# Selective scan on one Trainium2 core: the scan's last states copied by ScalarE, and the sum over directions made by identity products

## The chip, the core and the metric

The kernel runs on one core of a Trainium2 chip. The core has five instruction queues that run beside each other and meet through semaphores: TensorE (PE in the profile; its weight loads are PEld), VectorE (DVE), ScalarE (ACT), GpSimd (POOL) and SyncE (SP), which here issues the DMA transfers. Each queue runs its instructions in the order of the program. SBUF is the large on-chip memory; PSUM is the small one that TensorE writes its products to, and VectorE and ScalarE read and write it too.

The metric is the device time of one execution in microseconds (us), the median of several runs. The profile is one further execution, recorded by the hardware.

## What is computed

The reference is a network of two layers on 8 images of 128 channels and 64 x 64 places. The change touches the first layer's mixer alone, which runs a selective scan in four directions and sums the results:

```python
xp = x_norm @ in_w.T                                   # 4096 places, 128 channels
x_tb = xp.reshape(b, h, w, D).swapaxes(1, 2).reshape(b, L, D)
U = jnp.stack([xp, jnp.flip(xp, 1), x_tb, jnp.flip(x_tb, 1)], 0)
Y = jax.vmap(_mamba)(U, ...)                           # once for each direction

# in _mamba, for each direction: xh, z, dt, Bm, Cm are made from u, and then
h = exp(dt_t[..., None] * A) * h + (dt_t * x_t)[..., None] * B_t[:, None, :]
y = einsum('bdn,bn->bd', h, C_t)                       # 16 states a channel
y = (y + xh * Dp) * silu(z)
return y @ out_w.T

y_fused = gate[0] * y_lr + gate[1] * y_rl + gate[2] * y_tb + gate[3] * y_bt
out = skip_gate * (y_fused @ out_w.T) + (1.0 - skip_gate) * skip
```

Directions 1 and 3 read the sequence backwards, directions 2 and 3 read the image column by column. Their results are turned back before they are summed. Behind this come an expert layer and a whole second layer, which stay as they are.

## The kernel before

**Tiling.** The first layer is written by `scan_blocks` (L703). It goes through 8 images, in each through 4 directions `d`, in each through 4 chunks `j` of 1024 places, and in each chunk through 16 groups of 8 channels x 16 states = 128 partitions. A group of a chunk is a slot `n`; there are 2048 slots. The text numbers slots within their chunk, 0 to 15.

**A slot.** Slot `n` works ahead for its followers. For slot n+1 TensorE spreads dt over the states: six bf16 products into `dA` (two halves of 512 places, three bf16 parts each), and ScalarE takes the exponential in place. `dA` is a PSUM tile of two banks with two buffers. For slot n+2 GpSimd multiplies `xE` by B into `bx`; for slot n+4 SyncE fetches `xE`. For slot n itself VectorE runs the scan in place in `dA` (L765), starting from the column of `last` that the previous chunk left, then multiplies by C into `hc` (L335, the helper of all tensor-by-tensor operations), then copies the last column of `dA` into `last` for the next chunk (L772, helper L347). The fourth chunk of a direction copies nothing, so there are 3 x 16 x 32 = 1536 such copies. Every fourth slot TensorE sums the states of four `hc` tiles into the y bank (`y<-hc,kt`).

**The steps of a chunk.** What a chunk needs besides is a table of steps (L587) with the slot at which each is issued, counted from the chunk's first slot. Steps of several chunks and of the next image's input (`input_steps`, L605, in 8 of the 16 chunks of an image, for all but the last image) fall into one slot. Those that matter here, by the slot within a chunk in which they fall:

- slot 0: the products of D with x into the y bank (`skip`, 16), a dt product (`dt_product`), and a table load of ScalarE
- slot 1: `gate_y` (17): VectorE multiplies the y bank (two PSUM banks, 1024 places) by `zs`, the gated z
- slot 2: `out_product` (17.5: at the head of the slot, ahead of the slot's dA products) multiplies `zs` by the output weights and overwrites the y bank; `out_add` (18) brings the two halves of the y bank into `r`, the sum over directions that stays in SBUF. ScalarE also has softplus steps of a later chunk here (`plus_one`, `relu_abs`)
- slots 3 and 4: VectorE's and ScalarE's remaining softplus steps (`lost`, `ln`, `dt`)
- slots 4 to 6: the products that spread B and C and their copies by ScalarE
- slots 7 to 14: z products, z gates, convolution products (`taps`), x gates; in slot 12 of a direction's first chunk VectorE also makes `D_diag`.

`m` is a PSUM tile of one bank with two buffers, through which all the small products go; `y` has one buffer.

**The sum over directions.** For direction 0, `out_add` copies the y bank to `r` by ScalarE (L583). For the others VectorE adds it to `r` in place (L585, again shown as L335): forwards in order, reversed for d = 1, and through a view with a step of 64 elements (256 bytes) for d = 2 and 3, reversed for d = 3. `image_steps` (L676) adds the residual to `r` by GpSimd and stores it.

**What sets the order.** The tile framework sets the semaphores from what each instruction reads and writes. Besides, `ordered` (L307) chains the instructions of each engine, so that every queue runs exactly in the order in which the slots issue them:

```python
def ordered(self, i):
    if self.order is not None:
        e = i.ins.engine
        if e in self.order:
            self.after(i, self.order[e])
        self.order[e] = i
    return i
```

Within slot n the order of issue is: the steps at its head, the dA products and the exponential of slot n+1, `bx`, the fetch of `xE`, the scan, the C product and the copy of slot n, the y products, the other steps.

Of the kernel before, what the change touches and what calls it, by code (L numbers as in the profile page):

```python
# [12 lines left out]
ALU = mybir.AluOpType  # L13
# [9 lines left out]
L = 4096  # L23
S = 512
# [5 lines left out]
CH = 1024  # L30
NCH = L // CH
# [238 lines left out]
def bc(ap, n, axis=None):  # L270

    axis = len(ap.shape) if axis is None else axis
    v = ap.unsqueeze(axis)
    shape = list(v.shape)
    shape[axis] = n
    return v.to_broadcast(shape)


class Net:
# [167 lines left out]
    def scan_steps(self, ch, xp, r, pl, ps):  # L447
# [4 lines left out]
        nc, d, j = self.nc, ch["d"], ch["j"]  # L452
        pool = nc.gpsimd
        back = d % 2 == 1
        lo = L - CH * (j + 1) if back else CH * j
        dtb, cb2 = self.w(f"dt_b{d}"), self.cb2[:, d : d + 1]
        start = [lo + (1 - q if back else q) * S for q in range(2)]
        half = [slice(q * S, (q + 1) * S) for q in range(2)]
        ID, TANH = AF.Identity, AF.Tanh
        v = {}  # L460

        def order(ap):
            return ap[:, ::-1] if back else ap
# [5 lines left out]
        def make(name, bufs, width=S):  # L469
            t = v[name] = pl.tile([C, width], F32, name=name.rstrip("01"), bufs=bufs)  # L470
            return t
# [4 lines left out]
                o = start[q] + (6 - t if back else t)  # L476
                self.mm(p, self.Wt[:, d, t, :], xp[:, o : o + S], start=t == 0, stop=t == 3)

        def gate(name, to, q, **kw):
            p = v[f"{name}{q}"]  # L480
            self.act(order(to[:, half[q]]), p, ID, scale=0.5, **kw)
            th = make(f"th{q}", 2)
            self.act(order(th), p, TANH, scale=0.5, **kw)
            self.act(th, th, ID, bias=self.k("one"))

        def gated(of, name, q):
            to = of[name][:, half[q]]
            self.tt(to, to, v[f"th{q}"], ALU.mult, pool)

        def x_gate(q):  # L490
            if q == 0:
                ch["xs"] = make("xs", 3, CH)
            gate("x", ch["xs"], q, bias=cb2)

        def z_product(q):
            self.mm(bank(f"z{q}"), self.w(f"z_w{d}"), xp[:, start[q] + PAD : start[q] + PAD + S])
# [1 line left out]
        def z_gate(q):  # L498
            if q == 0:
                make("zs", 1, CH)  # L500
            gate("z", v["zs"], q)

        def dt_product(q):
            self.mm(bank(f"d{q}"), self.Wd[:, d, :], ch["xs"][:, half[q]])
# [58 lines left out]
                self.mm(ch["y"][rows_, half[q]], self.D_diag[:, rows_], ch["xs"][:, half[q]], start=False)  # L563

        def gate_y():
            self.tt(v["zs"], ch["y"], v["zs"], ALU.mult)

        def out_product(q):
            self.mm(ch["y"][:, half[q]], self.Wo[:, d, :], v["zs"][:, half[q]])

        def out_add(q):
            p, lo = ch["y"][:, half[q]], CH * j + q * S
            lo = L - S - lo if back else lo
            if d < 2:
                to = r[:, lo : lo + S]
                to = to[:, ::-1] if back else to
            else:
                w0 = lo // 64
                to = r.rearrange("p (h w) -> p w h", w=64)[:, w0 : w0 + S // 64, :]
                to = to[:, ::-1, ::-1] if back else to  # L580
                p = p.rearrange("p (w h) -> p w h", h=64)
            if d == 0:
                self.ordered(nc.scalar.copy(to, p))  # L583
            else:
                self.tt(to, to, p, ALU.add)  # L585

        table = [  # L587
            (-23, taps, 0, (0, 1)), (-22, taps, 0, (2, 3)), (-21, taps, 1, (0,)), (-20, taps, 1, (1,)),
            (-19, taps, 1, (2, 3)), (-21, x_gate, 0), (-18, x_gate, 1), (-20, gated, ch, "xs", 0), (-17, gated, ch, "xs", 1),
            (-16, dt_product, 0), (-15, dt_product, 1), (-16, self.table, EXP_LN_SET),  # L590
            (-15, relu_abs, 0), (-15, exp, 0), (-14, plus_one, 0), (-14, relu_abs, 1), (-13, exp, 1), (-13, plus_one, 1),
# [111 lines left out]
    def scan_blocks(self, r, xp, xt, pl, ps):  # L703

        nc = self.nc
        chunks = [{"d": d, "j": j} for b in range(self.nb) for d in range(4) for j in range(NCH)]
        per = NQ * 4 * NCH  # L710
        todo, ahead = {}, {}

        def plan(at, steps):
            for rel, step, *args in steps:
                slot = int(np.ceil(at + rel))
                (todo if slot == at + rel else ahead).setdefault(slot, []).append((step, args))

        for i, s in enumerate(range(NS)):
            plan(-56 - 7 * (NS - 1 - i), self.input_steps(0, s, xp, pl, ps, {
                "px": ("xE", 4), "pxc": ("hc", 5), "psq": ("bx", 4), "var": ("xs", 3), "q": ("C16", 2)}))  # L720
        plan(-24, [(0, self.table, EXP_TANH_SET)])
        for b in range(self.nb):
            plan(per * b, self.image_steps(b, r, xp, xt, pl))
            if b + 1 < self.nb:
                for i, s in enumerate((2, 3, 4, 5, 6, 7, 0, 1)):
                    plan(per * b + NQ * (5 + i), self.input_steps(b + 1, s, xp, pl, ps))
        for i, ch in enumerate(chunks):
            plan(NQ * i, self.scan_steps(ch, xp if ch["d"] < 2 else xt, r, pl, ps))
        total = NQ * len(chunks)
        self.order = {}  # L730
        self.table(EXP_LN_SET)
        total = NQ * len(chunks)
        self.order = {}
        self.table(EXP_TANH_SET)
        xE, bx, dA, hcs = {}, {}, {}, {}
        last = None
        for n in range(min(todo), max(todo) + 1):
            for step, args in ahead.pop(n, ()):
                step(*args)
            u = n + 1  # L740
            if 0 <= u < total:

                ch, q = chunks[u // NQ], 4 * (u % 4) + u % NQ // 4
                dA[u] = ps.tile([128, CH], F32, tag="dA", bufs=2, name="dA")
                sel = self.expand[:, 8 * q : 8 * q + 8, :].rearrange("p c n -> p (c n)")
                for h in range(2):
                    sg = slice(h * S, (h + 1) * S)
                    for i in range(3):
                        self.mm(dA[u][:, sg], sel, ch["parts"][:, i, sg], start=i == 0, stop=i == 2)
                self.act(dA[u], dA[u], AF.Exp, scale=self.negA[:, ch["d"] * NQ + q : ch["d"] * NQ + q + 1])  # L750
            u = n + 2
            if 0 <= u < total:
                bx[u] = pl.tile([128, CH], F32, name="bx", bufs=4)
                self.tt(bx[u], xE.pop(u), chunks[u // NQ]["B16"], ALU.mult, nc.gpsimd)
            u = n + 4
            if 0 <= u < total:
                ch, q = chunks[u // NQ], 4 * (u % 4) + u % NQ // 4
                xE[u] = pl.tile([128, CH], F32, name="xE", bufs=4)
                nc.sync.dma_start(xE[u], bc(ch["dtx"][8 * q : 8 * q + 8, :], NST, 1))
            if 0 <= n < total:  # L760
                ch, q = chunks[n // NQ], 4 * (n % 4) + n % NQ // 4
                if n % NQ == 0 and ch["j"] == 0:
                    last = pl.tile([128, NQ], F32, name="last", bufs=2)
                t = dA.pop(n)
                self.ordered(nc.vector.tensor_tensor_scan(  # L765
                    out=t, data0=t, data1=bx.pop(n), initial=0.0 if ch["j"] == 0 else last[:, q : q + 1],
                    op0=ALU.mult, op1=ALU.add,
                ))
                hcs[n] = pl.tile([128, CH], F32, name="hc", bufs=5)
                self.tt(hcs[n], t, ch["C16"], ALU.mult)  # L770
                if ch["j"] < NCH - 1:
                    self.copy(last[:, q : q + 1], t[:, CH - 1 :], nc.vector)  # L772
            if n % 4 == 0 and 4 <= n < total + 4:
                g0 = n - 4
                ch, k = chunks[g0 // NQ], g0 % NQ // 4
                if k == 0:
                    ch["y"] = ps.tile([C, CH], F32, tag="y", bufs=1, name="y")
                for h in range(2):
                    for g in range(4):
                        self.mm(ch["y"][32 * g : 32 * g + 32, h * S : (h + 1) * S],  # L780
                                self.k("collect")[:, 32 * k : 32 * k + 32],
                                hcs[g0 + g][:, h * S : (h + 1) * S], start=k == 0, stop=False)
                for g in range(4):
                    del hcs[g0 + g]
            for step, args in todo.pop(n, ()):
                step(*args)
        self.order = None
        self.silus_done([])
# [1127 lines left out]
```

## Time and profile before

| | us |
|---|---|
| median of 3 runs (18311.58 to 18333.5) | 18323.12 |
| the profiled execution | 18312.49 |
| its span in the profile | 18310.7 |
| first slot's scan starts, last slot's scan ends | 120.7, 8513.2 |

The groups of the page and of the trace that the change touches:

| operation | engine | count | busy, us | mean of one, ns |
|---|---|---|---|---|
| scan from a last state | VectorE | 1536 | 3609.4 | 2350 |
| scan from zero | VectorE | 512 | 1172.2 | 2289 |
| C product `hc` | VectorE | 2048 | 2508.0 | 1225 |
| copy of the last state | VectorE | 1536 | 226.5 | 147 |
| `gate_y` | VectorE | 128 | 155.4 | 1214 |
| add to `r` | VectorE | 192 | 196.9 | 1070 |
| copy to `r`, direction 0 | ScalarE | 64 | 34.2 | 591 |
| exponential | ScalarE | 2048 | 2229.6 | 1089 |
| output product | TensorE | 512 | 252.3 | 615 |

A group's busy time is the time in which one of its instructions ran, and the mean is that of one instruction. Instructions overlap: one can be issued before the one ahead of it has ended, so starts show the pace and durations do not. A product of fp32 operands of 512 columns is two matmul instructions. A row of the timeline gives the start, the length, the engine, the line, the operation with what it writes and reads, and how many were merged; in brackets stand the engine's idle time before it and what ended it.

### The profile page before, as it was taken

Reading aid. Unit: us, or ns where it says so; the run is one execution under the profiler, and the core shown is the slowest. Engines: PE = TensorE matmul, PEld = TensorE weight load, DVE = VectorE, ACT = ScalarE, POOL = GpSimd, SP = SyncE. Lnnn points to the kernel's source line nnn. Section 1 sums busy time; section 2 is a strip of 40 time slices with the busy share of each in tenths; the row PEclk is TensorE's granted clock in tenths of the full one; section 3 lists DMA queues with packets and bytes.
Section 4 is the critical chain, followed back from the end, with each engine's and each line's share of the span. In section 5 each row is a group of like instructions: output and inputs, shape, how many; then the busy total and the mean of one; then the engine's idle time right before and its main releaser. Section 6 shows DMA issues by size and latency. Waiting matters only on the chain. (4 is left out here: it accounts for less than half of the span.)

```text
span 18310.7 us, 298654 instructions
## 1 busy us (share of the span) xinstructions
PE 15555.4 (85%) x113015; PEld 8270.0 (45%) x114072; DVE 15183.5 (83%) x20469; ACT 11216.3 (61%) x15914; POOL 9304.0 (51%) x6309
## 2 busy tenths in 40 slices
PE   7777777777777777776687999999999999998998
PEld 2222222222222222223344677777777777774443
DVE  7999999999999999998464777777777777777886
ACT  5656666565666656554353677677767776776553
POOL 7878788787878788774111222222222222222444
PEclk9999999999999999998797999999999999998999
DMA  4555555555555555554541111111111111111222
GB/s 131 143 143 146 146 145 141 147 144 144 145 144 145 141 148 143 145 136 118 160 147 53 30 29 31 31 31 29 31 31 30 30 31 31 29 31 41 93 95 82
DMA packets 818996, 1735.35 MB, mean 95 GB/s; under 512 B 183571, under 2 KB 383667, under 8 KB 809139
## 3 DMA queue, kind: packets, MB, share of 16 engines
q1 hardware_dynamic: 817558, 1716.18, 32.8%
q8 instruction: 902, 14.78, 0.3%
q14 instruction: 536, 4.39, 0.1%
HBM read 1474.55 MB, written 241.30 MB: 94 GB/s over the span
## 5 line engine op out<-in xcount | busy, mean ns | idle before, releaser
L335 POOL TENSOR_TENSOR bx<-xE,B 128x1024 f32<-128x1024 f32 x2048 | 4808.6, 2357 | 342.8 <-DMA xE<-dtx_d 184.6
L288 PE MATMUL dA<-parts,expand 128*128 128x512 bf16 x11777 | 3168.4, 400 | 1753.3 <-DVE last L347 1307.1
L296 ACT ACTIVATE dA<-dA,negA 128x1024 f32<-128x1024 f32 x2048 | 2229.6, 1089 | 2962.2 <-PE dA L288 2954.8
L765 DVE TENSOR_TENSOR_SCAN dA<-dA,last,bx 128x1024 f32<-128x1024 f32 x1536 | 3609.4, 2350 | 91.2 <-ACT dA L296 78.5
L288 PEld LDWEIGHTS <-expand 128*128 128x128 bf16 x12288 | 1127.3, 100 | 4149.5 <-DVE last L347 2120.1
L344 DVE SCALAR_TENSOR_TENSOR E_cm<-E_cm,gm_cm 128x1024 f32<-128x1024 f32 x2048 | 2440.5, 1227 | 280.9 <-ACT E_cm L296 268.4
L335 DVE TENSOR_TENSOR hc<-dA,C 128x1024 f32<-128x1024 f32 x2048 | 2508.0, 1225 | 107.8 <-DVE dA L765 2.3
L1292 POOL COPY Sd_cm<-S_cm 64x128 f32<-64x128 f32 x1024 | 879.2, 859 | 2625.6 <-DVE S_cm L335 2536.6
L296 ACT ACTIVATE E_cm<-ss_p 128x1024 f32<-128x1024 f32 x2048 | 1980.7, 1021 | 267.5 <-PE ss_p L288 184.6
L335 POOL TENSOR_TENSOR xD_cm<-tok_cm,D_cm 128x256 f32<-128x256 f32 x512 | 404.2, 789 | 2377.2 <-PE y_p L288 2309.0
L288 PE MATMUL y_p<-E_cm,pad_cm 128*32 128x128 f32 x32768 | 1321.2, 277 | 119.8 <-DVE E_cm L344 118.6
L765 DVE TENSOR_TENSOR_SCAN dA<-dA,bx 128x1024 f32<-128x1024 f32 x512 | 1172.2, 2289 | 49.4 <-ACT dA L296 43.2
L288 PE MATMUL ss_p<-ssB_cm,ssA_cm 128*128 128x512 bf16 x3582 | 1041.0, 383 | 114.5 <-DVE gm_cm L335 45.9
L288 PE MATMUL y<-hc,kt 128*32 128x512 f32 x8192 | 1077.8, 646 | 3.7 <-DVE hc L335 3.6
L288 PEld LDWEIGHTS y_p<-E_cm,pad_cm 128*32 128x32 f32 x32768 | 903.6, 110 | 369.2 <-DVE E_cm L344 202.8
L288 PE MATMUL bc_p<-stk_cm,W_cm 128*128 128x256 f32 x4096 | 943.7, 384 | 26.3 <-DMA stk_cm<-in_ones_dram 20.6
L1149 DVE COPY dtr_cm<-tok_p 128x16 f32<-128x16 f32 x1024 | 176.5, 172 | 867.3 <-ACT tok_cm L296 867.3
L288 PEld LDWEIGHTS bc_p<-stk_cm,W_cm 128*128 128x128 f32 x4096 | 771.2, 191 | 167.5 <-issue 28.3
L288 PE MATMUL tok_p<-W_cm,stk_cm 128*128 128x200 f32 x4096 | 749.5, 336 | 0.0
L344 DVE SCALAR_TENSOR_TENSOR dw<-h,w_second,dw 128x512 f32<-128x512 f32 x1024 | 723.0, 748 | 1.2 <-ACT h L296 0.8
L296 ACT ACTIVATE tok_cm<-tok_p 128x384 f32<-128x384 f32 x1024 | 502.2, 490 | 347.8 <-DVE dtr_cm L1149 183.9
L288 PEld LDWEIGHTS tok_p<-W_cm,stk_cm 128*128 128x128 f32 x4096 | 683.1, 190 | 52.2 <-ACT BC_cm L296 48.1
(432 smaller groups left out, 29346.0 us busy)
## 6 DMA issues: line engine op xcount, KB each, us to landing
xE<-dtx_d SPq DMA_DIRECT2D x2048, 512.0 KB
dtx_d<-dtx SPq DMA_DIRECT2D x256, 256.0 KB
x<-x SPq DMA_DIRECT2D x256, 256.0 KB
pb<-p_d SPq DMA_DIRECT2D x64, 1024.0 KB
ssA_cm<-cs_cm SPq DMA_DIRECT2D x3072, 4.0 KB
stk_cm<-xs SPq DMA_DIRECT2D x368, 128.0 KB
stk_cm<-y SPq DMA_DIRECT2D x368, 128.0 KB
w<-in_w_dram SPq DMA_DIRECT2D x32, 1024.0 KB
```

The source lines that it names most:

```text
L288: return self.ordered(self.nc.tensor.matmul(out, lhsT=lhsT, rhs=rhs, start=start, stop=stop))
L296: i = self.ordered(self.nc.scalar.activation(out, in_, func, **kw))
L335: self.ordered((eng or self.nc.vector).tensor_tensor(out, a, b, op))
L344: self.ordered(self.nc.vector.scalar_tensor_tensor(out=out, in0=a, scalar=s, in1=b, op0=op0, op1=op1))
L765: self.ordered(nc.vector.tensor_tensor_scan(out=t, data0=t, data1=bx.pop(n), initial=0.0 if ch["j"] == 0 else last[:, q : q + 1], op0=ALU. ...
L1149: nc.vector.tensor_copy(dtr[:, c, jj, :], v[:, :, cfg.wsil :])
L1292: nc.gpsimd.tensor_copy(Sd[gr, :, g * hi : (g + 1) * hi], S2[gr])
```

## The change

Two things are changed, both in the first layer.

1. The last state is copied by ScalarE (`nc.scalar.copy`), and the copy is issued between the scan and the C product instead of behind the product by VectorE.
2. The sum over directions is made in the y bank: behind each output product a second product, by the identity, adds the old values of `r` to the same bank (directions 1 to 3), and ScalarE copies the bank to `r` in all directions. `r` is read and written in its own order, so the reversal of directions 1 and 3 moves ahead: `z_gate` no longer reverses, the halves of `zs` are swapped, and `gate_y` reads the y bank reversed.

```diff
-        def gate(name, to, q, **kw):
+        def gate(name, to, q, order=order, **kw):
             p = v[f"{name}{q}"]
-            self.act(order(to[:, half[q]]), p, ID, scale=0.5, **kw)
+            self.act(order(to), p, ID, scale=0.5, **kw)
...
         def gated(of, name, q):
-            to = of[name][:, half[q]]
+            to = of[name][:, half[1 - q if back and name == "zs" else q]]
...
-            gate("z", v["zs"], q)
+            gate("z", v["zs"][:, half[1 - q if back else q]], q, lambda ap: ap)
...
         def gate_y():
-            self.tt(v["zs"], ch["y"], v["zs"], ALU.mult)
+            self.tt(v["zs"], order(ch["y"]), v["zs"], ALU.mult)
+
+        def rows_of(ap, q):
+            at = lo + q * S
+            if d < 2:
+                return ap[:, at : at + S]
+            return ap.rearrange("p (h w) -> p w h", w=64)[:, at // 64 : (at + S) // 64, :]
+
+        def out_bank(q):
+            p = ch["y"][:, half[q]]
+            return p if d < 2 else p.rearrange("p (w h) -> p w h", h=64)
 
         def out_product(q):
-            self.mm(ch["y"][:, half[q]], self.Wo[:, d, :], v["zs"][:, half[q]])
+            self.mm(ch["y"][:, half[q]], self.Wo[:, d, :], v["zs"][:, half[q]], stop=d == 0)
+            if d:
+                self.mm(out_bank(q), self.k("ident"), rows_of(r, q), start=False)
 
         def out_add(q):
...
-            if d == 0:
-                self.ordered(nc.scalar.copy(to, p))
-            else:
-                self.tt(to, to, p, ALU.add)
+            self.ordered(nc.scalar.copy(rows_of(r, q), out_bank(q)))
...
                     op0=ALU.mult, op1=ALU.add,
                 ))
+                if ch["j"] < NCH - 1:
+                    self.ordered(nc.scalar.copy(last[:, q : q + 1], t[:, CH - 1 :]))
                 hcs[n] = pl.tile([128, CH], F32, name="hc", bufs=5)
                 self.tt(hcs[n], t, ch["C16"], ALU.mult)
-                if ch["j"] < NCH - 1:
-                    self.copy(last[:, q : q + 1], t[:, CH - 1 :], nc.vector)
```

More of the change, by code (lines that the diff above doesn't have):

```diff
@@ L492, in x_gate @@
                 ch["xs"] = make("xs", 3, CH)
-            gate("x", ch["xs"], q, bias=cb2)
+            gate("x", ch["xs"][:, half[q]], q, bias=cb2)
         def z_product(q):
@@ L565, in gate_y @@
         def gate_y():
-            self.tt(v["zs"], ch["y"], v["zs"], ALU.mult)
+            self.tt(v["zs"], order(ch["y"]), v["zs"], ALU.mult)
[7 more added lines that the diff above has]
+            return p if d < 2 else p.rearrange("p (w h) -> p w h", h=64)
         def out_product(q):
-            self.mm(ch["y"][:, half[q]], self.Wo[:, d, :], v["zs"][:, half[q]])
+            self.mm(ch["y"][:, half[q]], self.Wo[:, d, :], v["zs"][:, half[q]], stop=d == 0)
+            if d:
+                self.mm(out_bank(q), self.k("ident"), rows_of(r, q), start=False)
         def out_add(q):
[L572 to L576, printed above, removed]
-            else:
[L578 to L581, printed above, removed]
-            if d == 0:
-                self.ordered(nc.scalar.copy(to, p))
-            else:
-                self.tt(to, to, p, ALU.add)
+            self.ordered(nc.scalar.copy(rows_of(r, q), out_bank(q)))
         table = [
```

## The prediction

> **What bounds the kernel now.** First the page's header and its forty slices: is one engine full, and where?
>
> ```profile
> span 18310.7 us, 298654 instructions
> PE 15555.4 (85%) x113015; PEld 8270.0 (45%) x114072; DVE 15183.5 (83%) x20469; ACT 11216.3 (61%) x15914; POOL 9304.0 (51%) x6309
> ...
> DVE  7999999999999999998464777777777777777886
> ACT  5656666565666656554353677677767776776553
> ```
>
> The first layer is slices 1 to 19. There VectorE is full and ScalarE is not; asked for 110 to 8560 us, the table of windows gives VectorE 8139.6 of 8450 us (96%), TensorE 6587.9, GpSimd 6699.1, ScalarE 5089.2. So one reads VectorE's order next. The change touches this layer alone. Its 2048 slots (8 images x 4 directions x 4 chunks x 16 groups) take 4.10 us from scan to scan, 65.6 us a chunk. A slot with nothing extra looks so in the timeline:
>
> ```profile
> 3044.12 2.29 DVE L765 TENSOR_TENSOR_SCAN dA<-dA,bx 128x1024 f32<-128x1024 f32 x1
> ...
> 3044.26 1.47 PE L288 MATMUL dA<-parts,expand 128*128 128x512 bf16 x6
> ...
> 3045.77 1.09 ACT L296 ACTIVATE dA<-dA,negA 128x1024 f32<-128x1024 f32 x1 [0.47 <-PE dA L288]
> ...
> 3046.45 1.23 DVE L335 TENSOR_TENSOR hc<-dA,C 128x1024 f32<-128x1024 f32 x1
> ...
> 3047.59 0.15 DVE L347 COPY last<-dA 128x1 f32<-128x1 f32 x1
> 3047.65 2.29 DVE L765 TENSOR_TENSOR_SCAN dA<-dA,bx 128x1024 f32<-128x1024 f32 x1
> ```
>
> Scan and C product stand back to back; the copy of the last state lasts 0.15 us, but the scan after it starts 0.06 us behind it. The next slot's chain (matmuls, exponential) starts when the product frees a dA buffer and ends at 3046.86, **0.41 us after** this slot's product began. Nobody minds, as VectorE does not need it before 3047.65: two dA buffers hide that chain. Hold on to that 0.41.
>
> **Part 1: the copies of the last state.** 1536 leave VectorE. Their price there is not 226 us (1536 x 147 ns) but about 0.065 us each in start times (3.59 us a plain slot in chunks 1 and 2 against 3.52 in chunk 3, which copies nothing): 100 us gained at most.
>
> What is added is a reader of dA on another engine, between the scan and the product. Does the product then wait for it? Neither writes what the other reads. The second layer has just such a pair: ScalarE and VectorE read different columns of tok_p, a PSUM tile.
>
> ```profile
> 12007.98 0.49 ACT L296 ACTIVATE tok_cm<-tok_p 128x384 f32<-128x384 f32 x1 [0.54 <-PE tok_p L288]
> 12008.50 0.18 DVE L1149 COPY dtr_cm<-tok_p 128x16 f32<-128x16 f32 x1 [2.06 <-ACT tok_cm L296]
> 12008.71 1.05 ACT L296 ACTIVATE tok_cm<-tok_p 128x384 f32<-128x384 f32 x2 [0.24 <-DVE dtr_cm L1149]
> 12009.24 0.17 DVE L1149 COPY dtr_cm<-tok_p 128x16 f32<-128x16 f32 x1 [0.56 <-ACT tok_cm L296]
> ```
>
> The reads alternate strictly, in the order of the program, 0.03 us apart; ScalarE's second read waits for VectorE's first although it takes the other half of the tile (512 such waits in the tile's view, one for each second read). [...] So the product waits for ScalarE's copy.
>
> And that copy is queued **behind the exponential of the next slot**. Behind it stand the slot's own ScalarE steps and the exponential after that; behind the waiting product, VectorE's steps and the next scan. In the slot above, without the VectorE copy the matmuls start 0.06 earlier, the exponential ends at 3046.80. The copy's own time is not in the trace: 0.15 us as on VectorE, 0.205 as ScalarE's 128x4 row; I take 0.2, less the 0.07 by which ScalarE's instructions overlap (3042.45 + 1.09 against the next start at 3043.47). Then 0.03 to VectorE: product at 3046.96 instead of 3046.45. Less the copy's 0.06 the plain slot goes from 3.59 to about **4.03** (0.05 + 1.51 + 1.09 + 0.13 + 0.03 + 1.22): a loop through three engines instead of VectorE alone.
>
> Whatever delays matmul or exponential now stalls VectorE. From one product's end to the next, in slots of a copying chunk (now: scan starts averaged over chunks 0 to 2):
>
> - slots 5, 7, 9, 10, 11, 13, 14, 15: 29.1 us together, then 8 x 4.03: **+3.2**.
> - slot 0: TensorE has y products, D products and a dt product between two dA groups (3000.33 to 3006.26). 3.6, then 5.9: **+2.3**.
> - slot 1: gate_y 1.2, then both output products 1.8 ahead of the matmuls 1.5, exponential 1.1, copy, product. 5.45, then 7.0: **+1.5**.
> - slot 2: ScalarE must do the copy-out and three softplus steps (3.0 us; in 7 of 16 chunks also two powers, 1.2) before the exponential. Average 5.2, then 5.6: **+0.4**.
> - slot 3: VectorE's own softplus steps (2.7) cover the chain: **0**.
> - slot 4: the logarithm waits for the scan through the copy ahead of it, with two input steps in front in 7 of 16 chunks: **+0.5**.
> - slot 6: the second C spread product waits for a bank that ScalarE empties after its copy; with input steps 1.1 more: **+1.2**.
> - slots 8 and 12: y products and another product, 2.7 to 2.9 us against 2.5 of free TensorE: **+0.8** and **+0.5** (D_diag included).
>
> Sum 10.4 us a chunk.
>
> **Part 2: the sum over directions.** 192 adds leave VectorE: 0.64 us each in direction 1, 1.23 in directions 2 and 3.
>
> ```profile
> 3007.69 1.22 DVE L335 TENSOR_TENSOR zs<-y,zs 128x1024 f32<-128x1024 f32 x1
> ...
> 3008.96 1.98 PE L288 MATMUL y<-zs,W_out 128*128 128x512 f32 x4 [0.38 <-DVE zs L335]
> ...
> 3010.78 1.46 PE L288 MATMUL dA<-parts,expand 128*128 128x512 bf16 x6
> ...
> 3012.28 1.09 ACT L296 ACTIVATE dA<-dA,negA 128x1024 f32<-128x1024 f32 x1 [1.05 <-PE dA L288]
> ...
> 3012.49 2.45 DVE L335 TENSOR_TENSOR r<-r,y 128x512 f32<-128x512 f32 x2
> ...
> 3014.85 2.29 DVE L765 TENSOR_TENSOR_SCAN dA<-dA,bx 128x1024 f32<-128x1024 f32 x1
> ```
>
> The adds run beside a chain that ends at 3013.37, so without them the scan gains 1.5 us here, not 2.4. Direction 0, which adds nothing, shows what remains: slots 1 to 4 take 21.1 us (chunk 2), direction 1 21.5, directions 2 and 3 22.5; part is given back in slot 3, where ScalarE is late. The two identity products stand ahead of those matmuls: 4 instructions, 1.8 us at the price of the output products. In a chunk without copies of states that takes the gain back: about +1.0 in direction 1, 0 in 2 and 3. In a copying chunk they stand inside the loop: +1.8 in slot 1 in three of four directions, **+1.4** on average. What lay behind the adds is in slot 2's 5.2 already.
>
> [...] In directions 2 and 3 the identity product reads r every 256 bytes. The nearest row is the add with that stride: 1.23 for 0.64, two strided streams at 2.4 ns an element. TensorE takes 1.8 ns an element even contiguous (0.91 us for 512). [...] I take 0 for TensorE and keep 116 for the range. For ScalarE's strided write I take half a microsecond a copy over direction 0's 0.59, between 0 and 0.6; it is in slot 2.
>
> The reversal moved to gate_y, and the swapped halves of zs, cost nothing: the reversed adds of direction 1 took 0.64, no more than a forward 128x512 product (0.69); above, a doubling would be 64 x 1.2 = 77 us. No DMA moves. GpSimd adds the residual to r and SP stores r as before; GpSimd has a fifth of the layer free, more in longer slots.
>
> **Sum.** 10.4 + 1.4 = 11.8 us x 96 copying chunks = 1133; the other 24 chunks with an add: 8 x 1.0 = 8. The profiled execution took 18,312.5 us (span 18,310.7): 19,454. The median is 18,323, 11 more; I say **19,460 us**.
>
> **Rivals.**
> - *The readers are not ordered* (8%). Then VectorE gains 100 us, part 2 costs 1.0 x 32 = 32: 18,245, faster. It decides once the product starts at the scan's end. Against it: 512 waits at tok_p.
> - *The copy finds ScalarE free* (8%): only 0.03 + 0.2 + 0.03 - 0.06 a slot, 1536 x 0.2 = 307, plus 32: 18,650. Against it: the 0.41 above.
> - *TensorE cools* (7%). After 4.9 us of waiting six dA matmuls took 2.74 us (3018.51), not 1.47. [...] But groups of slots 0 and 1 average 1.8 now, after pauses of 2 us. If the 8 plain slots pay 1.27 each: 975 more, 20,430.
>
> **Chances.** The forecast keeps 77%, by itself 19,050 to 19,900 (116 for the stride, cold groups in three slots, some 370; less if copy and hand-offs are shorter). The range 18,900 to 19,950 reaches towards its neighbours. A measurement can tell about 0.2%, 37 us. The first rival is split between faster (7%) and the same (2%); all else is slower, 91%.
>
> **What would show it.** In the profile after: C products with idle time ended by ScalarE's copy, plain slots near 4.0 us, exponential, copy and product in a row, VectorE's busy share of the layer near 80%, output-product slots the longest. Products still at the scan's end would prove part 1 wrong; a group of four identity matmuls over 1.8 us, the stride.

## The result, and the profile after

| | before, us | after, us |
|---|---|---|
| median of 4 runs each | 18327.81 | 19574.38 |
| the profiled execution's span | 18310.7 | 19572.4 |
| first slot's scan to last slot's scan | 8390.2 | 9667.5 |
| a chunk whose slots copy states (mean of chunks 0 to 2) | 65.9 | 78.2 |
| a chunk whose slots copy none (chunk 3) | 64.7 | 67.5 |

The changed kernel is slower by 6.8%: ratio 1.0683, 95% interval 1.067 to 1.0697. The first layer grew by 1277 us and the whole span by 1262, so all of it is there. The last two rows are means of the scan starts in the traces.

The same parts of the page as before, its header and the forty slices (first layer: slices 1 to 20):

```profile
span 19572.4 us, 300377 instructions
PE 16127.2 (82%) x114456; PEld 8417.4 (43%) x114456; DVE 14852.7 (76%) x18741; ACT 11492.9 (59%) x17642; POOL 9307.0 (48%) x6309
...
DVE  6788788787887878788846567777777777776886
ACT  5555555555555555555426466777677677776553
PEclk8999999999998999999979799999999999999999
```

VectorE has lost the nines that marked it as the bound, and no other row has gained them: the layer is bound by no engine now, but by waiting between engines. VectorE is busy for 80% of it (6775.7 of 8450 us), the share that the prediction named. VectorE's work shrank by 331 us (15183.5 to 14852.7) and the kernel grew by 1262. What it waits for stands in the costliest groups of the page, first before, then after. The last columns are busy time, mean length in ns, and the engine's idle time ahead of the group with what ended it:

```profile
L335 DVE TENSOR_TENSOR hc<-dA,C 128x1024 f32<-128x1024 f32 x2048 | 2508.0, 1225 | 107.8 <-DVE dA L765 2.3
```

```profile
L335 DVE TENSOR_TENSOR hc<-dA,C 128x1024 f32<-128x1024 f32 x2048 | 2508.5, 1225 | 1673.8 <-ACT last L769 1646.9
```

The C product is no shorter or longer than before (1225 ns), but VectorE stood idle ahead of it for 1674 us, where before that was 108 us. The waits view counts 1536 such waits: one for each copied state. A plain slot in the timeline of the kernel after:

```profile
3349.91 2.35 DVE L764 TENSOR_TENSOR_SCAN dA<-dA,last,bx 128x1024 f32<-128x1024 f32 x1
3350.05 1.45 PE L288 MATMUL dA<-parts,expand 128*128 128x512 bf16 x6 [0.81 <-DVE hc L335]
...
3351.54 1.09 ACT L296 ACTIVATE dA<-dA,negA 128x1024 f32<-128x1024 f32 x1 [1.07 <-PE dA L288]
3352.56 0.16 ACT L769 COPY last<-dA 128x1 f32<-128x1 f32 x1
3352.75 1.23 DVE L335 TENSOR_TENSOR hc<-dA,C 128x1024 f32<-128x1024 f32 x1 [0.49 <-ACT last L769]
3353.89 2.35 DVE L764 TENSOR_TENSOR_SCAN dA<-dA,last,bx 128x1024 f32<-128x1024 f32 x1
```

Read it as a staircase: the previous product ends just before 3350, the matmuls start, then the exponential, then the copy, then the product. The scan ended at 3352.26, but the product began at 3352.75, behind a copy that stands in ScalarE's queue behind the exponential (and starts 0.07 us before that one's end). Scan to scan is 3.98 us, against 3.59 in the plain slots of chunks 1 and 2 before (3.53 in the slot shown of before, which is one of a first chunk).

And the output products of a chunk of direction 2 or 3, with old values of `r` added by TensorE:

```profile
3386.84 1.04 PE L288 MATMUL y<-zs,W_out 128*128 128x512 f32 x2
...
3387.71 1.87 PE L288 MATMUL y<-r,kt 128*128 128x512 f32 x2
...
3390.92 1.09 ACT L296 ACTIVATE dA<-dA,negA 128x1024 f32<-128x1024 f32 x1 [3.83 <-PE dA L288]
...
3392.11 2.36 DVE L764 TENSOR_TENSOR_SCAN dA<-dA,last,bx 128x1024 f32<-128x1024 f32 x1 [3.68 <-ACT dA L296]
...
3393.12 1.90 ACT L584 COPY r<-y 128x512 f32<-128x512 f32 x2
```

The identity product, two instructions like the output product, takes 1.87 us where that takes 1.04. The scan waited 3.68 us for an exponential that stands behind two output products and two identity products. (This output step falls into a chunk that copies no states, so the waiter is the scan and not the C product.)

### The profile page after: what moved, and what is told of

It reads as the page before. It is cut to its first block, busy times and chain, and to the rows that moved or that the text cites. A ratio compares the mean times of both kernels' runs of the same rounds, so it can differ in the third digit from the quotient of the medians.

```text
span 19572.4 us, 300377 instructions
## 1 busy us (share of the span) xinstructions
PE 16127.2 (82%) x114456; PEld 8417.4 (43%) x114456; DVE 14852.7 (76%) x18741; ACT 11492.9 (59%) x17642; POOL 9307.0 (48%) x6309
## 5 line engine op out<-in xcount | busy, mean ns | idle before, releaser
L288 PE MATMUL dA<-parts,expand 128*128 128x512 bf16 x12288 | 3279.4, 407 | 2230.8 <-DVE hc L335 2226.8
L335 DVE TENSOR_TENSOR hc<-dA,C 128x1024 f32<-128x1024 f32 x2048 | 2508.5, 1225 | 1673.8 <-ACT last L769 1646.9
L288 PE MATMUL ss_p<-ssB_cm,ssA_cm 128*128 128x512 bf16 x4096 | 1088.5, 383 | 70.6 <-DVE gm_cm L335 44.5
L288 PE MATMUL y<-hc,kt 128*32 128x512 f32 x8192 | 1131.9, 675 | 2.1 <-DVE hc L335 2.1
L335 POOL TENSOR_TENSOR dtx<-sp_r,xs 128x512 f32<-128x512 f32 x256 | 324.4, 1267 | 1071.8 <-DVE sp_r L335 1071.1
```

The source lines that it names most:

```text
L288: return self.ordered(self.nc.tensor.matmul(out, lhsT=lhsT, rhs=rhs, start=start, stop=stop))
L335: self.ordered((eng or self.nc.vector).tensor_tensor(out, a, b, op))
```

## The experiments

The prediction named two parts. The theory: the loss is the C product's wait for a copy that is queued behind the next exponential; the sum over directions costs little beside it. The rivals: the read order itself costs, or the second part costs as much. The first four runs share their runs of the kernel before (median 18319.4); the next four share theirs (18309.14); the last has 18322.24.

| run | us | ratio to before, 95% interval |
|---|---|---|
| part 1 alone | 19383.4 | 1.0578 (1.056 to 1.0595) |
| part 2 alone | 18623.4 | 1.0163 (1.0146 to 1.018) |
| part 1, exponential behind the copy | 18637.4 | 1.0173 (1.0156 to 1.019) |
| part 1, copy behind the product | 18517.8 | 1.0106 (1.009 to 1.0123) |
| part 1, copy untied | 18327.2 | 1.0011 (1.0002 to 1.0021) |
| part 2, no identity products | 18326.4 | 1.0009 (1.0 to 1.0019) |
| part 2, identity products contiguous | 18506.3 | 1.0108 (1.0093 to 1.0124) |
| before, copy by ScalarE in light slots | 18249.2 | 0.9971 (0.9959 to 0.9982) |
| part 2, no identity products, r contiguous | 18292.6 | 0.9988 (0.9977 to 0.9998) |

**Part 1 alone.** Against the kernel before:

```diff
+                if ch["j"] < NCH - 1:
+                    self.ordered(nc.scalar.copy(last[:, q : q + 1], t[:, CH - 1 :]))
                 hcs[n] = pl.tile([128, CH], F32, name="hc", bufs=5)
                 self.tt(hcs[n], t, ch["C16"], ALU.mult)
-                if ch["j"] < NCH - 1:
-                    self.copy(last[:, q : q + 1], t[:, CH - 1 :], nc.vector)
```

> Part 1 alone: the last states copied by ScalarE between scan and product, the sum over directions as before. Theory (the product waits for a copy that stands behind the next exponential): plain slots at 4.0 us as in the changed kernel, 11.1 us more in a copying chunk as its chunks of direction 0 show, 96 x 11.1 = 1070 us: about 19,400. Rival (the loss comes as much from the identity products inside the loop): well under 19,000.

1064 us more than before, as the theory had it. The second part adds only 191 us to this (19574.4 less 19383.4).

The longest step of a copying chunk is the one that holds the output products: from the end of product 1 to the end of product 2 it takes 8.2 us, against 5.4 before. The product's wait makes `gate_y` late, so TensorE waits too, and then runs slower:

```profile
2862.08 3.15 PE L288 MATMUL y<-zs,W_out 128*128 128x512 f32 x4 [2.80 <-DVE zs L335]
...
2865.02 2.04 PE L288 MATMUL dA<-parts,expand 128*128 128x512 bf16 x6
```

The same four output products took 1.98 us before, after a wait of 0.38 (3008.96). The table of windows gives the granted clock as the third number from the end, here for the output products before and in this run:

```profile
3008.96:3010.94 1.98, 1.98 (x5) 0.87 (x6) 1.98 (x1) 1.95 (x4) 0.15 (x1) 1.00 0.52 190
```

```profile
2862.08:2865.00 2.92, 2.92 (x4) 0.98 (x5) 2.21 (x1) 0.00 (x0) 0.63 (x1) 0.62 0.53 148
```

Over all copying chunks the output products take 2.70 us for 1.96 and the matmuls behind them 2.06 for 1.50 up to the exponential, at a mean granted clock of 0.75 and 0.76, where both had 1.00 before. That is 1.3 us a copying chunk, some 125 of the 1064 us. In the plain slots the clock stays at 1.00.

**Part 2 alone.** The changed kernel with the copies of the kernel before.

> Part 2 alone: sum by identity products, the last states copied by VectorE behind the product as before. By the prediction's sum 32 us, with the stride's doubling (identity products at 1.04 us an instruction in directions 2 and 3) some 150 us: 18,360 to 18,480. Rival (by the chunks of the changed kernel that copy nothing, which grew by 2.7 us in direction 1 and some 4 in 2 and 3): about 18,660, so more is lost at the output products than these products' own time.

304 us more: near the rival's number, not the prediction's. Where it loses, by slots (means of chunk 2): slot 2 went from 5.24 to 6.33 us, as the adds went and the identity products came, and slot 3 from 6.46 to 7.65, where the prediction had nothing for part 2. Slot 3 is also why part 2 is dearer by itself than on top of part 1 (191): in a copying chunk with part 1 it takes 6.4 us from product to product, with part 2 and without, so that its 1.2 us in 96 chunks, 116 us, are not lost there.

**Part 1, the exponential behind the copy.** In slot n, the exponential of slot n+1 is issued after the copy and not before the scan:

```diff
-                self.act(dA[u], dA[u], AF.Exp, scale=self.negA[:, ch["d"] * NQ + q : ch["d"] * NQ + q + 1])
+            exp_of = u
...
                     self.ordered(nc.scalar.copy(last[:, q : q + 1], t[:, CH - 1 :]))
+            if 0 <= exp_of < total:
+                ce, qe = chunks[exp_of // NQ], 4 * (exp_of % 4) + exp_of % NQ // 4
+                self.act(dA[exp_of], dA[exp_of], AF.Exp, scale=self.negA[:, ce["d"] * NQ + qe : ce["d"] * NQ + qe + 1])
+            if 0 <= n < total:
                 hcs[n] = pl.tile([128, CH], F32, name="hc", bufs=5)
```

> Part 1 alone, with the exponential of the next slot issued behind the copy instead of ahead of it. Theory (the price is the place behind the exponential): the product waits only for copy and hand-offs, plain slots 3.75 to 3.85 us, in sum 0.2 to 0.25 us for 1536 slots plus late ScalarE steps: 18,650 to 18,800. Rival (the order of the two reads itself costs what is lost, wherever the exponential stands): no nearer than 19,300.

Two instructions of one engine change places and 746 of the 1064 us are gone. The order of the two reads is still there, and a slot looks so:

```profile
3163.53 0.16 ACT L770 COPY last<-dA 128x1 f32<-128x1 f32 x1 [0.96 <-DVE dA L765]
3163.60 1.09 ACT L296 ACTIVATE dA<-dA,negA 128x1024 f32<-128x1024 f32 x1
3163.73 1.23 DVE L335 TENSOR_TENSOR hc<-dA,C 128x1024 f32<-128x1024 f32 x1 [0.23 <-ACT last L770]
```

Now ScalarE waits for the scan and copies at once; the product waits 0.23 us for copy and hand-offs, and the exponential runs beside it. Plain slots take 3.72 us, less than was expected. So the place in ScalarE's queue is most of the price, and the read order about 0.13 us a slot, after the 0.06 that VectorE saves. What else remains of the 318 us, over a third, lies mostly in slot 4 (5.98 for 4.92) and slot 7 (4.22 to 4.49 for 3.70), where ScalarE's steps come later than before.

**Part 1, the copy behind the product.** The kernel before, with its `self.copy(..., nc.vector)` made `self.ordered(nc.scalar.copy(...))` in its old place.

> Part 1 alone, with ScalarE's copy issued behind the C product. Theory (it is VectorE's wait that costs): VectorE waits for nobody, plain slots 3.52 us; the next matmuls in that dA buffer and ScalarE's steps wait 0.2 us longer, which two buffers hide: 18,200 to 18,400. Rival (ScalarE held up to the product's end makes exponentials late): over 18,500.

A miss for the theory as it was put: 198 us slower, the rival's side. No product waits any more and plain slots take 3.53 us, less than before, as expected. But the waits of VectorE show a new line-up:

```profile
DVE dA L765 <- ACT last L772: 214.4, 251, 3.3
DVE m L335 <- ACT sp_u L296: 123.7, 96, 2.0
DVE m L344 <- ACT sp_u L296: 85.1, 104, 0.8
```

(us in total, times, longest.) ScalarE is now held up to the end of the product, its softplus steps of slots 3 and 4 start later, and VectorE waits for those: slot 4 takes 6.2 us instead of 4.9, slot 3 7.0 instead of 6.4. Slot 7 takes 4.3 to 4.7 instead of 3.7, largely because of the first line. There the scan waits for an exponential that ScalarE reaches late; the view names the copy since that ended last (at 2642.43 in one such slot, the exponential at 2642.34, and the scan began at 2642.44). Elsewhere scans begin before the copy ahead of them, so they do not depend on it. A wait was taken from one engine and put on the other.

**Part 1, the copy untied.** Part 1 alone with `self.negA[:, q : q + 1]` copied in place of the column of `t`.

> Part 1 alone with the tie cut: ScalarE's copy stands where the change puts it, but reads a column of a constant in SBUF, so it waits for no scan and no product waits for it. The scan's state is not passed from chunk to chunk. Theory (the whole price is the product's wait): VectorE rid of 1536 copies at 0.065 us, 18,170 to 18,260. Rival (one more instruction on ScalarE makes exponentials and softplus steps late by itself): 18,320 or more.

The same 1536 instructions in the same place, and of 1064 us over the kernel before 18 are left (18327.2 less 18309.1): the tie is the loss. The gain that the theory put on top did not come, so the time is the rival's. Plain slots did go from 3.59 to 3.53 us, but slots 4 and 7 gave it back (5.23 for 4.92, 3.9 to 4.0 for 3.7), and so did slot 12 of the first chunks (5.78 for 5.16). VectorE's 100 us were worth nothing here, since one more ScalarE instruction stands ahead of steps that VectorE waits for: ahead of its scans it waited 184.6 us for ScalarE's exponential and copy (132.1 and 52.5), against 121.6 before.

**Part 2 without the identity products.**

```diff
-            self.mm(ch["y"][:, half[q]], self.Wo[:, d, :], v["zs"][:, half[q]], stop=d == 0)
-            if d:
-                self.mm(out_bank(q), self.k("ident"), rows_of(r, q), start=False)
+            self.mm(ch["y"][:, half[q]], self.Wo[:, d, :], v["zs"][:, half[q]])
```

> Part 2 alone without the identity products: directions are not summed, each overwrites r. Theory (part 2 loses by the 1.8 to 2.8 us of TensorE ahead of the next dA products): without them the adds' gain is left, 18,220 to 18,270. Rival (ScalarE's copies to r, ahead of its softplus steps, make those late and VectorE wait in slot 3): 18,350 or more.

Between the two: 17 us over the kernel before. Taking 197 us of adds off VectorE gained nothing. Slot 2 fell by 1.0 us (5.24 to 4.28 in chunk 2) and slot 3 rose by 1.2 (6.46 to 7.67). The waits of VectorE say to whom it went, first before, then in this run:

```profile
DVE m L344 <- ACT sp_u L296: 24.4, 53, 0.6
```

```profile
DVE m L344 <- ACT sp_u L296: 186.9, 126, 2.5
```

That is the softplus step waiting for ScalarE, which has the two copies to `r` ahead of its own softplus steps.

**Part 2 without identity products, `r` written without a step.** The same, with `r[:, lo + q * S : lo + q * S + S]` as the copy's target.

> Part 2 alone without the identity products, and ScalarE writing r without a step in all directions (directions are not summed, and 2 and 3 land in other places). Theory (ScalarE's strided copies at 1.09 us stand ahead of its softplus steps and make slot 3 long): 64 chunks times 2 copies times 0.5 us less than the run without identity products, about 64 us: 18,250 to 18,280. Rival (the two copies' place is enough, their length does not matter): 18,310 to 18,340.

34 us less, between theory and rival (against their own runs of before: 17 more and 30 less). Slot 3 of directions 2 and 3 fell by 0.7 us (8.54 to 7.82 in direction 2, chunk 2). Direction 1, whose copies are short in both runs, keeps its 7.82. So both count: the place of the copies (slot 3 of direction 1 took 6.44 us before), and the half microsecond by which the step lengthens each.

**Part 2, identity products contiguous.** Part 2 alone with `r[:, lo + q * S : lo + q * S + S]` as the moving operand.

> Part 2 alone, the identity products of directions 2 and 3 reading r without a step (other places are added than the reference adds); ScalarE still writes r with the step of 256 bytes. Theory (the step doubles these products and they stand in VectorE's way): 64 chunks times 1.9 us less than part 2 alone, 18,480 to 18,530. Rival (the added TensorE time of the step is hidden, ScalarE's strided writes cost the rest): 18,600.

117 us less than part 2 alone, or 107 when each is set against its own runs of the kernel before. First the instructions' lengths in the view of the tile `r`, of the changed kernel (shortest, median, longest in ns), then the same row of this run:

```profile
L288 PE MATMUL y<-r,kt x384: 592/1033/1061, 497.2 to 9803.5; 128*128 128x512 f32 x192
```

```profile
L288 PE MATMUL y<-r,kt x384: 592/592/593, 453.9 to 8715.8; 128*128 128x512 f32 x192
```

The step of 256 bytes lengthens the instruction from 592 to 1033 ns, and all of it lands on the time: 256 instructions in directions 2 and 3 times 0.44 us are 113 us. Part 2 alone is so taken apart, each run against its own runs of before: 17 us with the copies moved, 180 for the products themselves (18506.3 less 18326.4), 107 for their step, in sum 304.

**A faster version.** The kernel before with the copy by ScalarE, behind the product, where a slot has little ScalarE work that VectorE waits for:

```diff
-                    self.copy(last[:, q : q + 1], t[:, CH - 1 :], nc.vector)
+                    if n % NQ in (5, 8, 9, 10, 11, 12, 13, 14, 15):
+                        self.ordered(nc.scalar.copy(last[:, q : q + 1], t[:, CH - 1 :]))
+                    else:
+                        self.copy(last[:, q : q + 1], t[:, CH - 1 :], nc.vector)
```

> The kernel before, with ScalarE's copy behind the C product in slots 5 and 8 to 15 alone, where the run with all copies behind the product kept plain slots at 3.53 us against 3.59, and VectorE's copy in the others. Theory: 9 x 96 x 0.06 = 52 us less, and up to 1 us less for each of 32 D_diag: 18,230 to 18,280. Rival (ScalarE's wait for the product delays what follows in these slots too): 18,320 or more.

18249.2 us, 0.3% faster than the kernel before (0.9959 to 0.9982) and 6.8% faster than the changed one. But the copies are not what won it. Slots 8, 10, 11 and 12 take 3.53 us for 3.59 and slot 5 3.61 for 3.66, yet slots 7 and 13 give 0.1 to 0.2 back and others a little: as wholes, chunks 1 and 2 take 65.67 and 65.46 us, where before they took 65.66 and 65.47. The first layer shrank by 47 us in the trace, and 40 of them lie in slot 12 of the first chunks (3.92 for 5.16), with `D_diag`, of which the last section tells. So the 52 us that the theory put on the copies did not come, and that the time falls into its range is luck.

## Why the prediction was right, and where its sum was off

Of the some 115 us by which the time lies above the forecast, 66 belong to part 1 (1064 for 998) and 49 to part 2 (191 for 142).

**The mechanism was right.** The order of two reads, read off a pair of instructions in the second layer, holds in the first: 1536 waits for 1536 copies. The place behind the exponential was right and is now shown by exchanging the two. A plain slot was forecast at 4.03 us; slots 10, 11 and 14 take 3.98 to 4.00, while slot 5 takes 3.72 and slot 9 4.21. The copy takes 0.16 us where 0.2 was put.

**Part 1's sum was nearly right, and its shortfall has a place.** Forecast 10.4 us a copying chunk, measured 11.1 (1064 us over 96). Counted as the prediction counts, from one product's end to the next, in part 1 alone:

| slot | before, us | forecast | measured |
|---|---|---|---|
| 0 | 3.7 | 5.9 | 6.2 |
| 1 | 5.4 | 7.0 | 8.2 |
| 2 | 5.2 | 5.6 | 5.5 |
| 3 | 6.4 | as before | 6.4 |

Slot 1 is the mis-sized term: "both output products 1.8 ahead of the matmuls 1.5" ran in 2.70 and 2.06 us, as TensorE had waited for the gate (2.80 us in the step shown) and had a lower clock (0.75 and 0.76 on average). The prediction had that effect only as a rival for the plain slots and in its range. Slots 4 to 15 took 5.6 us more against 6.2: slots 6, 8 and 12 were put too high. These errors partly cancel.

**Part 2's term failed in size.** In copying chunks 1.4 us was forecast, and 1.3 is the difference between the changed kernel and part 1 alone (78.2 less 76.9), but that is luck. The identity products lengthen slot 1 by some 2.2 us with their step; 0.4 comes back because the matmuls behind them take 1.67 us and not 2.06, at a granted clock of 0.93, and 0.4 in slot 2 with the adds. In the chunks that copy nothing the prediction had "about +1.0 in direction 1, 0 in 2 and 3", in sum 8 us; by its own figures, 1.8 less a gain of 0.4 or 1.4, it should have had 1.4 and 0.4. They grew by 2.7, 5.3 and 2.8 us in directions 1 to 3, 87 us in all (64.7 to 67.5 on average). Two terms were mis-sized:

- "For ScalarE's strided write I take half a microsecond a copy", "it is in slot 2": the size was right (1.09 for 0.57 to 0.59 us), the place not. The copies stand ahead of softplus steps for which VectorE waits a slot later. The prediction had seen this in direction 0 ("part is given back in slot 3, where ScalarE is late") and did not carry it to the others. The adds' going was to leave a gain of some 100 us (by the prediction's figures 0.4 us in 32 chunks and 1.4 in 64); without the identity products the run was 17 us slower than the kernel before.
- The step of the identity product, of which the prediction said "I take 0 for TensorE and keep 116 for the range". No run shown ahead of the result gives the size of either. The runs give 107 to 117 us, at 1033 ns an instruction for 592, a factor of 1.75. So the zero was the wrong choice: the speed of an unstepped product did not tell what a step adds. The add with that very step, 1.23 us for 0.64, was the nearer row.

**The rivals.** Unordered readers: fallen by the 1536 waits. ScalarE free at the scan's end: fallen, that is the run with the exponential behind the copy, and its loss of 318 us is close to the 307 worked out for the copies, though over a third of it comes from late ScalarE steps. A cooling TensorE: fallen for the plain slots, which keep a median of 1.5 us from the first dA matmul to the exponential. Other products fill their pauses, so that in slots 8 to 14 TensorE typically stands for 1.7 us at most. It came true at the output products, after pauses of 2.8 us; there it is the 1.3 us a copying chunk of part 1. The granted clock of the whole fell from 0.955 to 0.942.

**Left open.** The two reads were kept in order in every run. What would happen without that order was not tried. No run kept TensorE's clock up at the output products, so the 1.3 us are read from the trace and not taken away by an experiment.

## What to carry to other kernels

Before an operation is moved to an engine with time to spare, ask what stands ahead of it in that engine's queue at that moment, and who then waits for it: here a copy of 0.16 us cost 1064 us since it was queued behind an exponential that two buffers had hidden until then. A second reader of a PSUM tile on another engine was a dependence in this kernel (1536 waits), and a tile of another layer showed it before anything was built (512). A wait can also be followed by a slower engine: TensorE's output products, behind waits of 2.8 us, took 2.70 us for 1.96 in part 1 alone, at a mean clock of 0.75. Time taken off the busiest engine (197 us of adds) gained nothing here where the engine that took it over is one that the busiest engine waits for a slot later.

## What had not been expected

TensorE's clock fell at the output products, which the forecast had at full speed. Behind a wait of 0.38 us the four of the kernel before ran 1.98 us at 1.00; behind 2.80 us those of part 1 alone ran 2.92 us at 0.63. The longest wait of which the prediction told, 4.42 us in the trace where it has 4.9, left six dA matmuls of the kernel before at 0.50 (2.74 us for 1.47). The length of the wait is not all: in the changed kernel the output products of two chunks stand behind 2.80 us each, and one group slows and the other does not:

```profile
1414.65 3.00 PE L288 MATMUL y<-zs,W_out 128*128 128x512 f32 x4 [2.80 <-DVE zs L335]
```

```profile
1491.81 1.98 PE L288 MATMUL y<-zs,W_out 128*128 128x512 f32 x4 [2.80 <-DVE zs L335]
```

The granted clock is 0.64 for the first and 1.00 for the second. What decides between the two was not shown.

`D_diag` is a VectorE operation on 128x128 elements in SBUF alone, with one input tile and a column of scalars. It took 0.45 to 4.39 us in the kernel before. Its end follows GpSimd's, as the timeline of the kernel before shows:

```profile
955.71 4.64 POOL L335 TENSOR_TENSOR bx<-xE,B 128x1024 f32<-128x1024 f32 x2
955.98 0.15 DVE L347 COPY last<-dA 128x1 f32<-128x1 f32 x1
956.05 4.39 DVE L339 TENSOR_SCALAR D_diag<-kt,w_first 128x128 f32<-128x128 f32 x1
```

Two GpSimd products run from 955.71 to 960.35, and `D_diag` ends 0.09 us after them. All 32 of them end 0.08 to 0.09 us after a GpSimd operation, in this kernel and in the changed one. In the run with copies in light slots the same one takes 0.48 us:

```profile
955.79 1.28 POOL L335 TENSOR_TENSOR xs<-xs,th 128x512 f32<-128x512 f32 x1
956.68 0.48 DVE L339 TENSOR_SCALAR D_diag<-kt,w_first 128x128 f32<-128x128 f32 x1
```

There too it ends 0.09 us behind a GpSimd operation (957.07), but that one is shorter and began 0.89 us ahead of it. The change of phase between the two engines took slot 12 of a first chunk from 5.16 to 4.42 us in the changed kernel as well, against the trend of all other slots: some 24 us of its time were won by an operation that the change does not touch. The trace shows the coincidence of the ends; its cause was not tested by itself.
